# Rows of two tiles in sixteen quads fetched one by one from SyncE and ScalarE in a two-layer relational graph convolution

## The chip, the cores and the metric

The kernel runs on one core of one Trainium2 chip. The metric is the device time in microseconds (us) of one execution; the time of a kernel is the median of its runs. The engines are PE (TensorE), DVE (VectorE), ACT (ScalarE), POOL (GpSimd) and SP (SyncE). SP computes nothing: it issues transfers. ACT and POOL can issue transfers too.

## The reference, cut to what matters

There are 12500 nodes with 128 features, 200000 edges sorted by destination, 8 relations and two layers. Each layer takes, for each destination node, the mean over each relation of the messages that arrive, and sums the means:

```python
W = jnp.einsum('rb,bio->rio', comp, basis)
xw = jnp.einsum('ni,rio->nro', x, W)
msgs = xw[src, et]
seg = dst * N_REL + et
summed = segment_sum(msgs, seg); cnt = segment_sum(ones, seg)
agg = (summed / maximum(cnt, 1)).reshape(N_NODES, N_REL, HIDDEN).sum(axis=1)
h_new = relu(agg + x @ root + bias);  h = h_new + h          # per layer
out = layernorm(x + h)
```

## The kernel before

The edges stand in 1563 tiles of 128 (the last has 64); Q = 4 tiles are a quad (NQ = 391 quads) and G = 8 tiles a group. For every tile the rows of its 128 source nodes must come into the 128 partitions of a buffer of the SBUF. `gather` does that on POOL: one indirect transfer a tile (line 583), at the row numbers that stand in one column of `idx` (layer 1, source x) or `idy` (layer 2, source y_d), and after each a memset of the tile `pace` (line 589), which nothing reads. A ring of 14 buffers of one quad each lets gathers go AHEAD = 12 quads ahead of their use.

Layer 1: for each tile DVE builds a one-hot matrix `dm` (`onehot`, line 873), weighted with the reciprocal counts; PE multiplies rows and `dm` into `s` (`means`, line 914); ACT copies `s` to `sT` (line 568, the helper `copy`); `product` (line 938) multiplies by the eight relation matrices into `y`; `place` (line 961) adds the result to its block of 128 nodes. `close_block` finishes a block: bias, relu and residual on DVE, a transpose (`turn`), the store of the transposed block to `hT_d`, then two halves (`half`, line 986) which multiply the block by all relation matrices of layer 2, and the store of 8 x 128 values a node to `y_d`. `open_block` and `turn_block` bring in the block's root part.

Layer 2 gathers rows of `y_d` (row = node x 8 + relation), so that each tile needs one matmul (`add_rows`, line 1028), accumulated over the tiles of a block; `finish` and `norm` do the rest and store `out`. The first gather of layer 2 waits for the stores of all blocks of `y_d`.

The order of the work is that of the program text: every helper (`vec`, `act`, `pe`, `pool`, `load`) adds an instruction to a list, `Plan`, which works out the semaphore waits by what each one reads and writes, and each engine runs its own instructions in the order of the list. Transfers of `load` (line 565) go out on SP, or at the start on ACT. A transfer takes one of a fixed number of semaphores (a "lane"), in turn, and waits for the lane's previous transfer. The main loop over the quads of layer 1 starts at line 1117, what follows it at 1148, layer 2 at 1160. Other lists that matter: `todo` holds the steps `turn`, `half(0)`, `half(1)` of closed blocks, one of which is taken in most quads. `src_i` holds the source node of each edge with 128 edges of a tile along a row: tile i is row i % 128 of block i // 128; `idx` is its transpose.

After the last instruction all engines meet, POOL drains (line 1185), and a flag `bad` is loaded into a register of every engine (line 1212): if the edges broke an assumption, a general path would run. It doesn't here.

Of the kernel before, what the change touches and what calls it, by code (L numbers as in the profile page):

```python
# [415 lines left out]
def ordered_path(  # L416
# [21 lines left out]

    nc = tc.nc
    P = 128
    N, D = x.shape
# [16 lines left out]
    C = P + 2 * HALO  # L460
    S4 = 4
    AHEAD = 12
    H = R // 2
    assert D == P and R * K == P and B == BF + 1 and 1 < TL and LAST < P and BF % 4 == 0
    main = slice(HALO, HALO + P)

    const = ctx.enter_context(tc.tile_pool(name="const", bufs=1))
# [36 lines left out]
    sel = keep([P, G, K], F32, "sel")  # L504
    spread = keep([P, B, GB], F32, "spread")

    PACE, PACED = 8, (2 * P, 200)
    pace = keep([P, PACE, 2 * P], F32, "pace")
    paced = tc.alloc_semaphore("s_paced")
    key = keep([P, 4, C], F16, "key")  # L510
    low = keep([P, 4, C], I32, "low")
    eqs = Ring(const, 2, [P, S4, 4, C], F16, "eq")
    turns = Ring(const, 3, [P, 4, P], F32, "tu")
    rows_r = Ring(const, AHEAD + 2, [P, Q, D], F32, "rows")
    dm_r = Ring(const, 4, [P, Q, 2 * P], F32, "dm")
    sT_r = Ring(const, 3, [P, R, G, K], F32, "sT")
    pl_r = Ring(const, 3, [P, 2 * P], F32, "pl")
# [27 lines left out]
    o2 = keep([P, B], F32, "o2")  # L545
    nb_f = keep([1, 1], F32, "nb_f")

    plan = Plan(tc, {"hw": 8, "aq": 4, "gq": 3})
    plan.seen, plan.last = {}, {}

    def vec(emit, reads=(), writes=()):
# [15 lines left out]
    def copy(out_t, in_t, reads, writes):  # L567
        act(lambda: nc.scalar.activation(out_t, in_t, AF.Copy), reads, writes)  # L568

    rows_g = {}  # L570

    def gather(l, q):
        if q >= NQ:
            return
        t, cell = rows_r.take()
        rows_g[l, q] = (t, cell)
        ids = idx if l == 0 else idy

        def emit():
            ins = []  # L580
            for i in range(q * Q, min((q + 1) * Q, T)):
                m = LAST if i == T - 1 else P
                ins.append(nc.gpsimd.indirect_dma_start(  # L583
                    out=t[:m, i - q * Q, :], out_offset=None, in_=x if l == 0 else y_d,
                    in_offset=bass.IndirectOffsetOnAxis(ap=ids[:m, i:i + 1], axis=0)))
                k = l * T + i
                if k >= PACE:
                    nc.gpsimd.wait_ge(paced, k - PACE + 1)
                nc.gpsimd.memset(pace[:, k % PACE, :PACED[l]], 0).then_inc(paced, 1)  # L589
            return ins  # L590

        b = q * Q // P
        reads = ["idx0" if l == 0 and q == 0 else ("idx", b)] if l == 0 else [("idy", b)]
        if l == 1 and q == 0:
            reads += [("y_d", j) for j in range(NT)]
        plan.add("POOL", emit, reads, [cell], lane="gq", n=min(Q, T - q * Q))

    def weight(l, r):
        c0 = (l * R + r) * NB
# [306 lines left out]
    def means(q):  # L906
        t, c = rows_g.pop((0, q))
        d, dc = dms.pop((0, q))
        s, sc = s_b[q % 2]

        def emit():
            for i in range(in_quad(q)):
                m = LAST if q * Q + i == T - 1 else P
                last = nc.tensor.matmul(s[:, i, :], t[:m, i, :], d[:m, i, :P], start=True, stop=True)  # L914
            return last

        pe(emit, [c, dc], [sc])
        g = q * Q // G
        if g not in sT:
            sT[g] = sT_r.take()  # L920
        o, oc = sT[g]
        k0 = q * Q - g * G
        n = in_quad(q)
        copy(o[:, :, k0:k0 + n, :].rearrange("p r t k -> p t r k"),
             s[:, :n, :].rearrange("p t (r k) -> p t r k", k=K), [sc], [oc + (q % 2,)])
# [43 lines left out]
    def close_block(j):  # L969
        n = rows_of(j)  # L970
        p, pc = po[j]
        t, c = h_in.pop(j)
        h, hc = h_r.take()
        vec(lambda: nc.vector.tensor_add(h[:n], p[:n], bias_sb[:n]), [pc, "bias"], [hc])  # L974
        vec(lambda: nc.vector.scalar_tensor_tensor(h[:n], h[:n], 0.0, t[:n], op0=ALU.max, op1=ALU.add), [c], [hc])
        pt, pc2 = pt_b
        yc, ycc = yc_r.take()
        yr, yrc = yr_r.take()

        def turn():  # L980
            pe(lambda: nc.tensor.transpose(pt[:, 0, :n], h[:n, :], ident[:n, :n]), [hc, "ident"], [pc2])
            copy(yc[:, :n], pt[:, 0, :n], [pc2], [ycc])
            load(hT_d[j * P:(j + 1) * P, :n], yc[:, :n], [ycc], [("hT_d", j)])

        def half(k):
            pe(lambda: nc.tensor.matmul(pt[:n].rearrange("p r d -> p (r d)"), yc[:, :n],  # L986
                                        w_sb[:, 1, k * H:(k + 1) * H, :].rearrange("p r d -> p (r d)"),
                                        start=True, stop=True),
               [ycc] + [("w", 1, r) for r in range(k * H, (k + 1) * H)], [pc2])
            copy(yr[:n, k * H:(k + 1) * H, :], pt[:n], [pc2], [yrc + (k,)])  # L990
            if k == 1:
                load(y_d[j * P * R:(j * P + n) * R, :].rearrange("(p r) d -> p (r d)", r=R),
                     yr[:n].rearrange("p r d -> p (r d)"), [yrc + (0,), yrc + (1,)], [("y_d", j)])

        todo.extend([turn, lambda: half(0), lambda: half(1)])
# [7 lines left out]
             (ct_b[0].rearrange("p t d -> p (t d)")[:, :2 * P], ct_b[1])]  # L1003

    def load2(k):
        if not 0 <= k < NT:
            return
        n = rows_of(k)
        t, c = hTs[k] = hin_r.take()
        load(t[:, :n], hT_d[k * P:(k + 1) * P, :n], [("hT_d", k)], [c])  # L1010
        t, c = xs[k] = xs_r.take()
        load(t[:n], x[k * P:k * P + n, :], [], [c])

    def add_rows(q, k, opens, last):
# [2 lines left out]
        a, ac = acc[k]  # L1017
        n = in_quad(q)
        root_in = opens and k >= 0
        reads = [c, dc]  # L1020
        if root_in:
            ht, hc = hTs[k]
            reads += [hc, ("w", 1, R)]
# [1 line left out]
        def emit():  # L1025
            for i in range(n):
                m = LAST if q * Q + i == T - 1 else P
                ins = nc.tensor.matmul(a, t[:m, i, :], d[:m, i, :], start=(opens and i == 0),  # L1028
                                       stop=(last and i == n - 1))
                if i == 0 and root_in:  # L1030
                    nc.tensor.matmul(a[:, :rows_of(k)], w_sb[:, 1, R, :], ht[:, :rows_of(k)], start=False, stop=False)
# [63 lines left out]
        gather(0, q)  # L1095
    load_block(0)
    load_block(1)
    run(counts(0), 99)
    sources(*groups[1])
    turn_block(0)  # L1100
# [13 lines left out]
    later = [lambda b=b: check_edges(b) for b in range(B)]  # L1114
    later += [check_span, check_place, check_all]
    later.reverse()
    for q in range(NQ):
        g = q * Q // G
        gather(0, q + AHEAD)
        onehot(0, q + 2)  # L1120
        if q == 1:
            where()
# [8 lines left out]
        else:  # L1131
# [3 lines left out]
            for j in fresh(g):  # L1135
                if j not in hT:
                    turn_block(j)
                load_block(j + 1)
        if q % 4 != 3 and todo:
            todo.pop(0)()  # L1140
        if q < R:
# [3 lines left out]
                parts = None  # L1145
        elif later:
            later.pop()()
    g = NG - 1
    for j in place(g - 1):
        close_block(j)  # L1150
    product(g)
    place_in(g)
    while todo:
        todo.pop(0)()
    for j in place(g):
        close_block(j)
    while todo:
# [2 lines left out]
    for q in range(AHEAD):  # L1160
        gather(1, q)
    load2(0)
    for q in range(2):
        onehot(1, q)
    due = []
    for q in range(NQ):
        k = sup(q)
        gather(1, q + AHEAD)
        onehot(1, q + 2)
        opens = q == 0 or sup(q - 1) != k  # L1170
        last = q == NQ - 1 or sup(q + 1) != k
        if opens:
            acc[k] = acc_b[k % 3]
            load2(k + 1)
        add_rows(q, k, opens, last)
        for d in due:
            norm(d)
        due = []
        if last:
            finish(k)  # L1180
            due.append(k)
# [60 lines left out]
```

## Time and profile before

| | |
|---|---|
| median of 3 runs | 4566.05 us (4556.4 to 4580.39) |
| profiled execution | 4497.58 us |
| span of its instructions | 4495.7 us |
| POOL busy | 3928.1 us (87%) |
| PE busy | 2752.1 us (61%) |
| DVE busy | 1711.8 us (38%) |
| ACT busy | 518.9 us (12%) |
| indirect transfers of a tile, each layer | 1563 |
| DMA share: indirect queue, hardware queue 1 | 17.5%, 5.9% |
| moved | 295.88 MB, mean 66 GB/s |

The page's first part gives each engine's busy time; the second cuts the span in 40 slices with the busy share of each in tenths; the chain follows the work that ended last back from the end, at each step to what released it. In the groups, each line names the code line, engine, operation, output and inputs, how often, then the busy time and the mean of one in ns, and last the idle time ahead of them and what ended most of it. A name with a q (SPq, ACTq, POOLq) is the engine's own queue of instructions: transfers that it issues, register work and waits. "issue" is time in which an engine waited for nothing that the profile shows.

### The profile page before, as it was taken

To read this page: it belongs to the slowest core of one execution; us is meant where nothing else is said; L and a number is where in the kernel's file an instruction comes from. 1 tells how busy PE (TensorE), PEld (TensorE's weight loads), DVE (VectorE), ACT (ScalarE), POOL (GpSimd) and SP (SyncE) were. 2 spreads that over 40 slices of the span, in tenths; PEclk is the share of its full clock that TensorE was granted. 3 is DMA by queue.
4 is the path that set the end of the run, shared out by engine and by line. 5 is a ranking of instruction groups with operands and counts; after the bars stand their busy time and mean duration, and the time that the engine had idled before them with its cause. 6 is when DMAs were issued, how large, how long until landed. Compare 5 with 4: busy or idle time off the path is not lost.

```text
span 4495.7 us, 38109 instructions
## 1 busy us (share of the span) xinstructions
PE 2752.1 (61%) x11691; PEld 2130.6 (47%) x11691; DVE 1711.8 (38%) x4724; ACT 518.9 (12%) x1190; POOL 3928.1 (87%) x6260
## 2 busy tenths in 40 slices
PE   4786666666666666666656565565655556555554
PEld 3565555555555555555544444444444444444443
DVE  8772222222222222222234444444444444444343
ACT  0231121112111111121110000000000000000000
POOL 8888888888888888888878888888888888888886
PEclk7998888888888887888876666666666666666677
DMA  3232222222222222222222222222222222222221
GB/s 90 68 89 73 75 75 75 75 75 75 70 75 75 75 75 75 75 74 72 75 64 56 56 56 56 56 56 56 56 56 56 56 56 56 56 56 56 56 56 44
DMA packets 193416, 295.88 MB, mean 66 GB/s; under 512 B 60725, under 2 KB 130687, under 8 KB 193203
## 3 DMA queue, kind: packets, MB, share of 16 engines
q0 software_dynamic: 100032, 205.00, 17.5%
q1 hardware_dynamic: 90650, 86.62, 5.9%
q8 instruction: 96, 1.57, 0.2%
q10 hardware_dynamic: 2521, 1.73, 0.1%
q14 instruction: 117, 0.96, 0.1%
HBM read 229.11 MB, written 64.00 MB: 65 GB/s over the span
## 4 chain that ended last, share of the span: by engine, by line
POOL 72%; issue 10%; PE 10%; DVE 4%; DMA 4%; ACT 0%; POOLq 0%; ACTq 0%; DVEq 0%; SPq 0%
POOL rows L583 55%; POOL pace L589 17%; PE y L938 3%; DMA rows<-in_x_dram,idx 2%; PE s L914 2%; PE s L1028 2%; DMA rows<-y_d,idy 1%; DVE w_sb L607 1%; PE ct L1028 1%; DVE dm L873 1%; DVE eq L709 1%; PE ct L715 1%; PE ct L716 1%; PE pt L986 0%; DVE tu L732 0%
## 5 line engine op out<-in xcount | busy, mean ns | idle before, releaser
L583 POOL DMA_INDIRECT rows<-y_d,idy x1563 | 1486.6, 951 | 280.2 <-issue 254.8
L583 POOL DMA_INDIRECT rows<-in_x_dram,idx x1563 | 1494.5, 956 | 258.8 <-issue 249.5
L1028 PE MATMUL s<-dm,rows 128*128 128x256 f32 x2086 | 840.8, 567 | 599.1 <-DMA rows<-y_d,idy 445.9
L914 PE MATMUL s<-dm,rows 128*128 128x128 f32 x3126 | 539.7, 326 | 714.7 <-DMA rows<-in_x_dram,idx 714.4
L1028 PEld LDWEIGHTS s<-dm,rows 128*128 128x128 f32 x2086 | 560.9, 285 | 842.4 <-issue 444.1
L589 POOL MEMSET pace<- 128x256 f32 (+1 forms) x3126 | 953.3, 305 | 1.9
L914 PEld LDWEIGHTS s<-dm,rows 128*128 128x128 f32 x3126 | 467.1, 228 | 896.2 <-DMA rows<-in_x_dram,idx 760.1
L873 DVE TENSOR_SCALAR dm<-cols,near,w 128x256 f32<-128x256 f32 x1563 | 725.8, 534 | 56.4 <-PE ct L1028 28.9
L873 DVE TENSOR_SCALAR dm<-cols,kr,w 128x128 f32<-128x128 f32 x1563 | 531.4, 402 | 468.7 <-PE s L914 468.7
L1028 PE MATMUL ct<-dm,rows 128*128 128x256 f32 x1040 | 412.9, 560 | 306.0 <-DMA rows<-y_d,idy 235.0
L938 PE MATMUL y<-w_sb,sT 128*128 128x128 f32 x3136 | 562.1, 356 | 0.0
L938 PEld LDWEIGHTS y<-w_sb,sT 128*128 128x128 f32 x3136 | 553.0, 273 | 0.3 <-issue 0.2
L1028 PEld LDWEIGHTS ct<-dm,rows 128*128 128x128 f32 x1040 | 276.7, 282 | 427.5 <-issue 230.0
L974 DVE TENSOR_TENSOR h<-po,bias_sb 128x128 f32<-128x128 f32 x98 | 28.5, 291 | 944.7 <-PE po L961 944.7
L568 ACT ACTIVATE sT<-s 128x512 f32<-128x512 f32 x391 | 233.3, 597 | 1190.1 <-PE s L914 1189.5
L1047 DVE TENSOR_TENSOR y_col<-s,hT 128x128 f32<-128x128 f32 x66 | 19.2, 291 | 605.0 <-ACT hT L1040 605.0
L986 PE MATMUL pt<-w_sb,y_col 128*128 128x512 f32 x392 | 210.2, 618 | 2.1 <-ACT y_row L568 1.4
L1063 DVE TENSOR_TENSOR h<-po,xs 128x128 f32<-128x128 f32 x98 | 28.6, 292 | 303.8 <-PE po L1062 303.8
L1040 ACT ACTIVATE hT<-s,bias_t 128x128 f32<-128x128 f32 x65 | 23.9, 367 | 997.5 <-PE s L1028 997.5
L568 ACT ACTIVATE y_row<-pt 128x512 f32<-128x512 f32 x196 | 117.0, 597 | 140.4 <-PE pt L986 140.4
L961 PE MATMUL po<-ys,pl 128*128 128x128 f32 x780 | 119.8, 276 | 5.3 <-DVE pl L949 3.1
L1047 DVE TENSOR_TENSOR y_col<-ct,hT 128x128 f32<-128x128 f32 x32 | 9.3, 292 | 291.8 <-ACT hT L1040 291.8
(121 smaller groups left out, 1301.1 us busy)
## 6 DMA issues: line engine op xcount, KB each, us to landing
y_d<-y_row SPq DMA_DIRECT2D x97, 512.0 KB
rows<-in_x_dram,idx POOLq DMA_INDIRECT x1563
rows<-y_d,idy POOLq DMA_INDIRECT x1563
h_in<-in_x_dram SPq DMA_DIRECT2D x98, 64.0 KB
h_in<-hT_d SPq DMA_DIRECT2D x98, 64.0 KB
xs<-in_x_dram SPq DMA_DIRECT2D x98, 64.0 KB
hT_d<-y_col SPq DMA_DIRECT2D x97, 64.0 KB
out_dram<-ys SPq DMA_DIRECT2D x97, 64.0 KB
```

Of the source, the lines that this page charges most:

```text
L568: act(lambda: nc.scalar.activation(out_t, in_t, AF.Copy), reads, writes)
L583: ins.append(nc.gpsimd.indirect_dma_start(out=t[:m, i - q * Q, :], out_offset=None, in_=x if l == 0 else y_d, in_offset=bass.IndirectOffse ...
L589: nc.gpsimd.memset(pace[:, k % PACE, :PACED[l]], 0).then_inc(paced, 1)
L607: vec(lambda b=b: nc.vector.scalar_tensor_tensor(w_sb[:, l, r, :], b_sb[:, l, b, :], comp_sb[:, c0 + b:c0 + b + 1], w_sb[:, l, r, :], op0= ...
L709: vec(lambda s=s, eq=eq, s0=s0: nc.vector.tensor_tensor(eq[:, s - s0, :nb, HALO - s:HALO + P], key[:, :nb, HALO - s:HALO + P], key[:, :nb, ...
L715: nc.tensor.matmul(ct[:, :nb, :], id_h, eq[:, s - s0, :nb, main], start=(s == 1), stop=False)
L873: last = nc.vector.tensor_scalar(t[:, i - q * Q, :wide], cols[:, :wide], ids[:, i:i + 1], w[:, i:i + 1], op0=ALU.is_equal, op1=ALU.mult)
L914: last = nc.tensor.matmul(s[:, i, :], t[:m, i, :], d[:m, i, :P], start=True, stop=True)
L938: last = nc.tensor.matmul(y[:m], t[:, r, :nt, :].rearrange("p t k -> p (t k)"), w_sb[:, 0, r, :], start=(r == 0), stop=(r == R - 1))
L961: last = nc.tensor.matmul(po[j][0][:n], t[:m, k * P:k * P + n], o[:m], start=False, stop=(j in closed))
L986: pe(lambda: nc.tensor.matmul(pt[:n].rearrange("p r d -> p (r d)"), yc[:, :n], w_sb[:, 1, k * H:(k + 1) * H, :].rearrange("p r d -> p (r d)"),
L1028: ins = nc.tensor.matmul(a, t[:m, i, :], d[:m, i, :], start=(opens and i == 0), stop=(last and i == n - 1))
```

## The change

Of every 64 tiles, two no longer come by an indirect transfer from POOL. Tile 63 of the 64 comes over SP and, from the second 64 on, tile 31 over ACT (`far` tells which; in all 24 tiles on SP and 23 on ACT in each layer). `fetch` brings them in bites of 8 rows, one bite on each queue in each quad: the engine loads 8 row numbers from `src_i` into 8 registers, and issues 8 transfers of one row (512 bytes) each at an address from a register; each address takes a fused register instruction ahead of its transfer. A far tile is complete 8 quads (LEAD) before its quad is multiplied. It has a buffer of its own, two for each engine. On ACT in layer 1 the bite is cut in two: register load and 4 rows early in the quad, 4 rows late.

For layer 2 one DVE instruction turns `src_i` into row numbers of `y_d`. The first far tile of each queue in layer 2 waits for all stores of `y_d`.

Besides, the steps at the end of layer 1 stand in another order: `product`, `place` and `close_block` of the group before the last, and all but one of the steps left in `todo`, come ahead of the last quad's `means`. The last block's second half goes to the bank `ct` instead of `pt`, is copied by DVE, and each half is stored by itself. Layer 2 loads two blocks ahead at its start; the last quad's `add_rows` comes after the `norm` of the block before; and POOL gets a drain right after its last gather.

The core of the diff (the reads of `add_rows`, the assertion, and lines that only rename are left out):

```diff
+    FAR, LEAD = 16, 8
+    BITE = P // FAR
+    far_r = {e: Ring(const, 2, [P, D], F32, f"far{e}") for e in ("SP", "ACT")}
-    plan = Plan(tc, {"hw": 8, "aq": 4, "gq": 3})
+    plan = Plan(tc, {"hw": 8, "aq": 4, "gq": 3, "rSP": 4, "rACT": 4})
+    far_at = {"SP": FAR - 1, "ACT": FAR // 2 - 1}
+    row_regs = {e: [plan.engines[e].alloc_register(f"row{k}") for k in range(BITE)] for e in far_at}
+    def far(i):
+        for e, at in far_at.items():
+            if i % (FAR * Q) == at * Q + Q - 1 and i < BF * P and (at == FAR - 1 or i >= FAR * Q):
+                return e
+        return None
+
+    def fetch(e, l, q, part=0, parts=1):
+        s = q + LEAD + FAR - 1 - far_at[e]
+        i, c = (s // FAR * FAR + far_at[e]) * Q + Q - 1, s % FAR
+        if far(i) != e:
+            return
+        if c == 0 and part == 0:
+            far_g[l, i] = far_r[e].take()
+        t, cell = far_g[l, i]
+        n = BITE // parts
+        eng = plan.engines[e]
+        regs = row_regs[e]
+
+        def emit():
+            if part == 0:
+                eng.load(regs, src_i[i % P:i % P + 1, i // P, c * BITE:(c + 1) * BITE])
+            ins = []
+            for k in range(part * n, part * n + n):
+                at = eng.snap(regs[k], min_val=0, max_val=(N if l == 0 else N * R) - 1)
+                p = c * BITE + k
+                ins.append(eng.dma_start(t[p:p + 1, :], (x if l == 0 else y_d)[bass.ds(at, 1), :]))
+            return ins
...
+        tiles = [i for i in range(q * Q, min((q + 1) * Q, T)) if not far(i)]
...
+                rows = far_g[0, q * Q + i][0] if far(q * Q + i) else t[:, i, :]
+                last = nc.tensor.matmul(s[:, i, :], rows[:m], d[:m, i, :P], start=True, stop=True)
...
+            hb, hc2 = ct_b if j == NT - 1 and k == 1 else pt_b
...
+            if j == NT - 1:
+                if k == 0:
+                    copy(yr[:n, :H, :], hb[:n], [hc2], [yrc + (k,)])
+                else:
+                    vec(lambda: nc.vector.tensor_copy(yr[:n, H:, :], hb[:n]), [hc2], [yrc + (k,)])
+                load(y_d[...][:, k * H:(k + 1) * H, :], yr[:n, k * H:(k + 1) * H, :], ...)
+                return
...
+    for s in range(LEAD):
+        fetch("SP", 0, s - LEAD)
+        fetch("ACT", 0, s - LEAD)
...
-    for q in range(NQ):
+    for q in range(NQ - 1):
         g = q * Q // G
         gather(0, q + AHEAD)
+        fetch("SP", 0, q)
+        fetch("ACT", 0, q, 0, 2)
...
+        fetch("ACT", 0, q, 1, 2)
...
+    vec(lambda: nc.vector.scalar_tensor_tensor(src_i[:, :BF], src_i[:, :BF], float(R), ex[:, :BF, main], ...))
     g = NG - 1
+    while todo:
+        todo.pop(0)()
+    place_in(g - 1)
+    for j in fresh(g - 1):
+        open_block(j)
+    product(g - 1)
     for j in place(g - 1):
         close_block(j)
+    place_in(g)
+    while len(todo) > 1:
+        todo.pop(0)()
+    means(NQ - 1)
+    todo.pop(0)()
     product(g)
-    place_in(g)
...
     for q in range(NQ):
         k = sup(q)
         gather(1, q + AHEAD)
+        if q + AHEAD == NQ - 1:
+            pool(lambda: nc.gpsimd.drain())
+        fetch("SP", 1, q)
+        fetch("ACT", 1, q)
         onehot(1, q + 2)
```

## The prediction

> **What bounds the kernel now.** First the page: busy shares, slices, chain and costliest groups.
>
> ```profile
> PE 2752.1 (61%) x11691; PEld 2130.6 (47%) x11691; DVE 1711.8 (38%) x4724; ACT 518.9 (12%) x1190; POOL 3928.1 (87%) x6260
> POOL 8888888888888888888878888888888888888886
> POOL 72%; issue 10%; PE 10%; DVE 4%; DMA 4%; ACT 0%; POOLq 0%; ACTq 0%; DVEq 0%; SPq 0%
> L583 POOL DMA_INDIRECT rows<-y_d,idy x1563 | 1486.6, 951 | 280.2 <-issue 254.8
> L583 POOL DMA_INDIRECT rows<-in_x_dram,idx x1563 | 1494.5, 956 | 258.8 <-issue 249.5
> L589 POOL MEMSET pace<- 128x256 f32 (+1 forms) x3126 | 953.3, 305 | 1.9
> L568 ACT ACTIVATE sT<-s 128x512 f32<-128x512 f32 x391 | 233.3, 597 | 1190.1 <-PE s L914 1189.5
> ```
>
> POOL is busy evenly from start to end; its two gather lines and the pace memset carry the chain. Its idle time is "issue", 0.16 us a gather: it waits for nobody. Next the waits, then POOL in order of time in layer 2.
>
> ```profile
> POOL rows L583 <- issue: 504.3, 3057, 0.2
> POOL rows L583 <- DMA y_d<-y_row: 22.3, 1, 22.3
> ```
> ```profile
> 3000.30 0.95 POOL L583 DMA_INDIRECT rows<-y_d,idy  x1 [0.17 <-issue]
> 3001.25 0.28 POOL L589 MEMSET pace<- 128x200 f32 x1
> 3001.69 0.95 POOL L583 DMA_INDIRECT rows<-y_d,idy  x1 [0.17 <-issue]
> ```
>
> The one real stall is 22.3 us between the layers. The pitch of a gather in layer 2 is (4468.77 - 2288.24)/1562 = 1.396 us by the first and last gathers; in layer 1, by the starts 1435.75 and 1447.28 eight gathers apart, 1.441 us. So a layer is 1563 pitches, and everything else fits under it. SP and ACT have room: ACT is 12% busy and its sT copies wait for PE most of the time, and SP's own waits (2043.7, 1078.5 and 1067.2 us for DVE and ACT results) fill nearly all its time.
>
> The new work needs prices for register loads, register arithmetic and one-partition transfers. The instructions of single lines and of the tiles ex and dx show a few (duration min/median/max in ns):
>
> ```profile
> L1212 SPq TENSOR_LOAD <-bad x1: 467/467/467, 4489.0 to 4489.0; - x1
> L1212 SPq FUSED_REGOPS  x1: 191/191/191, 4493.6 to 4493.6; - x1
> L1185 POOLq DRAIN  x1: 8477/8477/8477, 4480.5 to 4480.5; - x1
> L565 ACTq DMA_DIRECT2D dx<-in_dst_dram x1: 257/257/257, 18.5 to 18.5; - x1
> L565 SPq DMA_DIRECT2D h_in<-hT_d x99: 320/433/459, 2284.9 to 4433.6; - x99
> ```
>
> The 257 ns one is the last dx load, a single partition; the last ex load, also one partition, is the 289 ns minimum of its group. Transfers over 128 partitions take 320 alone and 433 back to back.
>
> [...]the DMA engines are 17.5 + 5.9 + 0.4 = 24% busy.[...]the trace has 467 ns for one register, and no load of eight.[...]
>
> **The change part by part.**
>
> *Gathers removed.* 24 tiles a layer go to SP (63, 127, ... 1535) and 23 to ACT (95, ... 1503). POOL loses 47 gathers and 47 memsets a layer: 47 x 1.441 = 67.7 and 47 x 1.396 = 65.6, together 133 us. POOL's layers become 1516 pitches, 2185 and 2116 us.
>
> *Rows added.* For every quad of four tiles each queue gets one bite: a load of 8 registers, then 8 times a fused register instruction and a one-partition transfer. Call its price F. A row: transfer 0.28 (between 0.257 and 0.289, plus a little for a register address; bounds 0.26 to 0.43), register arithmetic 0.10 (bounds 0.05, near a plain branch at 0.038 to 0.05, and 0.19, the one record, which is the first of its kind after a barrier[...]), two gaps of 0.04 as between SP's back-to-back transfers: 0.46. The load: 1.0 us[...], an estimate. F = 8 x 0.46 + 1.0 = 4.7 us[...].
>
> SP, 384 bites a layer, has besides some 98 x 3 transfers of 0.43 = 126 us: 384 x 4.7 + 126 = 1931, under 2116. ACT, 368 bites, has in layer 1 its copies: sT 233, y_row 117, ys 54, hT 27, y_col 27, together 458 us if nothing overlaps[...]: 368 x 4.7 + 458 = 2188, just at 2185[...]. In layer 2 ACT's copies are 70 us. So both queues fit under POOL, SP at 0.91[...]. The cover is thin: it is gone on SP in layer 2 from F = (2116 - 126)/384 = 5.2, on ACT in layer 1 from 4.7 (serial)[...]. Above that each 0.1 us of F costs 37 to 38 us a layer.
>
> *What is queued behind.* On SP, hT_d, y_d, h_in, xs and out loads stand behind bites, and PE waits for h_in and hT; on ACT, the copies of sT stand behind half a bite (layer 1) and PE waits to reuse s and for product. A layer starts with 8 bites in a row on SP, 8 x 4.7 = 38 us. POOL runs up to 12 quads, about 67 us, ahead of PE, and a far tile is complete 8 quads before its use, so such delays are absorbed if the queues catch up; the last 15 quads of a layer have no bite. Cost nothing while F stays under the limits.
>
> *The wait between layers.* The chain there ran from the last gather at 2264.72 to POOL's restart at 2288.24. Product of the last but one group (3.21), its place and one or two of the y halves now precede the last rows' arrival; the last y goes in two banks with two copies and two stores. What remains after the rows land (2267.06): last means 1.1, one half with 1.2, product 1.9, ys copy and place 0.8, adds 0.6, transpose and copy 0.7, two halves 2.2, copy 0.6, store 3.3, restart 0.7: 2280.2. Gain 8 us, bounds 3 and 11. The DVE multiply of src_i over 1536 columns, about 3 x 0.68 = 2.1 us by the tu group's record, runs while DVE waits for rows. Two moved steps at the end of layer 2 gain about 1 us, not counted.
>
> *The drain.* POOL's drain of 8.5 us starts at 4480.5, after everything, though POOL was done at 4470.0. A drain right after the last gather starts there and ends about 4478.5, beside PE's and DVE's last work; if the second drain finds nothing left, 8 us go. Bounds 0 (the second costs the same) and 9; I take 8[...].
>
> Sum: 133 + 8 + 8 = 149 us; span 4495.7 - 149 = 4347, execution 4497.58 - 149 = 4349. The median of the runs shown, 4566.05, is 1.0152 times the profiled execution; scaled alike, 4415 us, 3.3% faster.
>
> **Rivals.**
>
> *A queue becomes the bound and the kernel is slower.* For it: the only recorded register instruction is 0.19 us[...]. With the row at 0.28 + 0.19 + 0.08 = 0.55 and the load at 1.0, F = 5.4. ACT with serial copies then needs 368 x 5.4 + 458 = 2445 in layer 1, SP 384 x 5.4 + 126 = 2200 in layer 2; with 35 us around the layers (51 before, less 16) the span is 4680, 184 longer, and the time 4753 us. It decides where the sum passes 4495.7: with serial copies at F = (4495.7 - 35 - 458 - 126)/752 = 5.15, with copies that overlap fully (SP alone in both layers) at (4495.7 - 35 - 252)/768 = 5.5.[...] Against it: [...]the copies may overlap.
>
> *Part of the gain is eaten.* F = 5.0 with serial copies on ACT: layer 1 takes 368 x 5.0 + 458 = 2298, layer 2 stays at 2116: 4449, 47 us gained, 4518 us.
>
> *One DMA engine fills up.* If all 12032 rows go to one engine, 2 packets each at the hardware queue's mean (5.9% of 16 x 4495.7, over 90650 packets: 0.047 us) are 1.13 ms, 26% on top of 24%: no bound. It decides from (1 - 0.24) x 4347/12032 = 0.27 us a row; the indirect queue's mean packet, 0.126, would give 0.25. Above it PE waits for rows and the time is over 4566. Few in a hundred.
>
> *The change doesn't do it.* If POOL's pitch were set by how fast transfers drain, fewer gathers would each take longer, leaving the 16 us at the ends: about 4550. Against it: 0.95 + 0.28 + 0.17 makes the pitch, with no wait.
>
> **How the numbers follow.** POOL still sets the time: 0.47, 4415 us, own range 4385 to 4440 (ends' bounds 3 to 20 us). Partly eaten: 0.20, 4440 to 4540. Nothing changed: 0.05. A queue or DMA engine bound, slower: 0.28, of which half lies below 4680. The range 4385 to 4680 leaves about 0.14 above and 0.04 below. The three runs of this kernel lie 0.5% apart, so less than 23 us can't be told from no change: faster 0.67, same 0.05, slower 0.28.
>
> **What would show it.** Right: 1516 gathers a layer at pitches 1.44 and 1.40, no POOL wait longer than the one between layers, and that near 14 us; SP's register instruction near 0.1, its transfer near 0.28, the load near 1.0; a short second drain. Wrong: POOL waiting for PE in each layer's later part, PE waiting for farSP or farACT rows, ACT or SP without idle time[...].

## The result, and the profile after

The changed kernel takes 5226.03 us (median of 4 runs, 5209.97 to 5237.52) against 4568.49 us before (4 runs): a ratio of 1.1437, 95% interval 1.139 to 1.1484. It is 14% slower where 3% faster was forecast. This holds for the chip on which these runs were timed. On another chip the same kernel later took 4370.49 us beside 4498.56, a ratio of 0.9713 (0.9696 to 0.9729). The kernel before splits the chips in the same way: it takes 4556 to 4586 us on some and 4497 to 4500 on others, and nothing between. Below, a chip of the first sort is called tight, one of the second roomy. All executions told of here were recorded by the profiler while they ran. Runs made together, on one chip, are called a job.

The page of the changed kernel, from the tight chip: the span, the busy shares, POOL's slices, the chain by engine and by line, and the two gather groups.

```profile
span 5215.7 us, 75611 instructions
PE 2512.0 (48%) x11691; PEld 2052.8 (39%) x11691; DVE 1710.9 (33%) x4726; ACT 522.6 (10%) x1189; POOL 3819.4 (73%) x6072
POOL 8688888888888888884676667666676666666764
SPq 43%; issue 34%; ACTq 9%; PE 6%; DVE 3%; another core or an unknown queue 2%; ACT 1%; DMA 1%; DVEq 0%
L630 POOL DMA_INDIRECT rows<-y_d,idy x1516 | 1444.9, 953 | 922.0 <-PE po L1121 624.5
L630 POOL DMA_INDIRECT rows<-in_x_dram,idx x1516 | 1454.5, 959 | 418.8 <-issue 214.5
```

POOL's work went as planned: 1516 gathers a layer, each as long as before (953 and 959 ns against 951 and 956). But POOL is no longer in the chain; SP's own queue has 43% of it, and POOL's slices drop from 8 to 6 and 7 in layer 2. Next the waits of several engines, in us in total, times, and the longest; the last line is SP's own longest sum:

```profile
ACT hT L1099 <- DMA farACT<-y_d: 1086.5, 48, 63.9
PE s L1087 <- DMA h_in<-hT_d: 952.8, 53, 20.9
POOL rows L630 <- PE po L1121: 624.5, 91, 33.6
POOL rows L630 <- DMA y_d<-y_row: 59.8, 1, 59.8
SPq L572 <- ACT y_col L575: 61.0, 8, 31.6
```

ACT's copies wait behind the row transfers of its own queue (first line); PE waits for h_in, an ordinary load that stands on SP behind the rows; POOL waits for PE to give buffers back; the wait between the layers grew from 22.3 to 59.8 us. SP itself hardly waits any more: its longest sum is 61.0 us, for y_col, where before it waited over 4000 us in all. So SP's queue sets the pace. The instructions of the row lines on SP tell why (duration min/median/max in ns, then the first and last start):

```profile
L601 SPq TENSOR_LOAD <-src_i x768: 3/734/1677, 18.8 to 5170.6; - x192
L604 SPq FUSED_REGOPS  x6144: 1/44/839, 19.6 to 5174.9; - x199
L606 SPq MOVE farSP<-y_d x3072: 1/29/831, 2431.8 to 5174.9; - x192
L606 SPq DMA_DIRECT2D farSP<-y_d x3072: 1/226/817, 2431.9 to 5175.0; - x192
```

The medians are low: 44 + 29 + 226 ns and the gaps make 0.42 us a row. But the maxima of all four kinds are near 0.8 us or above, even of a MOVE that normally takes 29 ns. The minima are as strange: 2134 of SP's 6144 row transfers are recorded as shorter than 50 ns, where none takes less than 224 in the same kernel on the roomy chip. So the record of an instruction's start may come late, too: an inference from these minima, which no run tested. From the instruction records, the mean distances from one instruction to the next add up to 0.63 us a row in layer 1 and 0.78 in layer 2. In long stretches both SP and ACT advance only once in some 0.70 us, at the same moments, twice in a gather's pitch of 1.39 us, whatever the instruction is: ends on SP at 3023.14, 3024.66, 3025.41, 3026.83 and 3028.26 us, on ACT at 3023.13, 3024.62, 3025.41, 3026.82 and 3028.26. Sorted by what POOL was doing: in layer 2, from one transfer of a bite to the next, a row on SP took 0.93 us while gathers were being issued and 0.42 while none had come for 2 us. First to last gather, layer 1 took 2367.2 us (before 2261.3) and layer 2 2731.1 (before 2180.5).

### The profile page after: what moved, and what is told of

It is laid out like the page before. It is cut to its first block, busy times and chain, and to the rows that moved or that the text cites. A ratio compares the mean times of both kernels' runs of the same rounds, so it can differ in the third digit from the quotient of the medians.

```text
span 5215.7 us, 75611 instructions
## 1 busy us (share of the span) xinstructions
PE 2512.0 (48%) x11691; PEld 2052.8 (39%) x11691; DVE 1710.9 (33%) x4726; ACT 522.6 (10%) x1189; POOL 3819.4 (73%) x6072
## 2 busy tenths in 40 slices
DMA packets 214575, 298.19 MB, mean 57 GB/s; under 512 B 71235, under 2 KB 152973, under 8 KB 214069
## 4 chain that ended last, share of the span: by engine, by line
SPq 43%; issue 34%; ACTq 9%; PE 6%; DVE 3%; another core or an unknown queue 2%; ACT 1%; DMA 1%; DVEq 0%
SPq L606 26%; SPq L604 8%; SPq L601 7%; ACTq L606 6%; SPq L572 2%; ACTq L604 2%; DVE dm L921 1%; PE s L1087 1%; ACTq L601 1%; PE s L963 1%; PE y L987 1%; DVE w_sb L655 1%; DMA h_in<-hT_d 1%; PE pt L1036 1%
## 5 line engine op out<-in xcount | busy, mean ns | idle before, releaser
L630 POOL DMA_INDIRECT rows<-y_d,idy x1516 | 1444.9, 953 | 922.0 <-PE po L1121 624.5
L630 POOL DMA_INDIRECT rows<-in_x_dram,idx x1516 | 1454.5, 959 | 418.8 <-issue 214.5
L1087 PE MATMUL s<-dm,rows 128*128 128x256 f32 x2024 | 626.2, 462 | 1150.6 <-DMA h_in<-hT_d 952.8
L1087 PEld LDWEIGHTS s<-dm,rows 128*128 128x128 f32 x2024 | 453.8, 237 | 1266.1 <-issue 568.0
L1087 PE MATMUL ct<-dm,rows 128*128 128x256 f32 x1008 | 307.6, 457 | 618.8 <-DMA h_in<-hT_d 551.4
L963 PEld LDWEIGHTS s<-dm,rows 128*128 128x128 f32 x3032 | 511.1, 245 | 116.7 <-issue 109.4
L987 PEld LDWEIGHTS y<-w_sb,sT 128*128 128x128 f32 x3136 | 512.4, 255 | 45.4 <-ACT sT L575 23.1
L1087 PEld LDWEIGHTS ct<-dm,rows 128*128 128x128 f32 x1008 | 222.6, 233 | 676.4 <-issue 272.8
L1036 PE MATMUL pt<-w_sb,y_col 128*128 128x512 f32 x390 | 257.0, 746 | 72.5 <-ACT y_col L575 52.6
L1010 PEld LDWEIGHTS po<-ys,pl 128*128 128x128 f32 x780 | 115.2, 212 | 368.5 <-ACT ys L575 289.0
L940 PE MATMUL pt<-ident,h_in 128*128 128x128 f32 x98 | 40.5, 414 | 315.6 <-DMA h_in<-in_x_dram 231.5
```

Of the source, the lines that this page charges most:

```text
L630: ins.append(nc.gpsimd.indirect_dma_start(out=t[:m, i - q * Q, :], out_offset=None, in_=x if l == 0 else y_d, in_offset=bass.IndirectOffse ...
L963: last = nc.tensor.matmul(s[:, i, :], rows[:m], d[:m, i, :P], start=True, stop=True)
L987: last = nc.tensor.matmul(y[:m], t[:, r, :nt, :].rearrange("p t k -> p (t k)"), w_sb[:, 0, r, :], start=(r == 0), stop=(r == R - 1))
L1010: last = nc.tensor.matmul(po[j][0][:n], t[:m, k * P:k * P + n], o[:m], start=False, stop=(j in closed))
L1036: pe(lambda: nc.tensor.matmul(hb[:n].rearrange("p r d -> p (r d)"), yc[:, :n], w_sb[:, 1, k * H:(k + 1) * H, :].rearrange("p r d -> p (r d)"),
L1087: ins = nc.tensor.matmul(a, rows[:m], d[:m, i, :], start=(opens and i == 0), stop=(last and i == n - 1))
```

## The experiments

The theory after this trace (A): the gathers fill something that every instruction of SP and ACT needs as well. The rivals: the rows are simply dearer than priced (B); SP and ACT hinder each other, or the changed ends cost the time; later, that layer 2 is slow for a cause of its own.

**The ends alone, half the rows, SP alone, and prices by stage (tight chip, before 4568.15).** The ends alone:

```diff
     def far(i):
-        for e, at in far_at.items():
-            if i % (FAR * Q) == at * Q + Q - 1 and i < BF * P and (at == FAR - 1 or i >= FAR * Q):
-                return e
         return None
```

> No far tiles at all: all 1563 gathers of a layer stay on POOL, only the other order of the last steps, the split last store and the earlier drain remain. Every theory: layers as before (pitch 1.441 and 1.396 us), wait between the layers near 14 us instead of 22.3, second drain short; 12 to 17 us less than before, ratio 0.996 to 0.998. If the ends carried part of the loss (a new wait between the layers, 59.8 us in the changed kernel), 20 us or more longer than before.

Measured: 4546.58 us, ratio 0.9957 (0.9943 to 0.9971), 22 us less. The ends gain; the loss is the rows'. The run's own trace misses the expectation in two places, though: layer 2 took 2216.3 us and not 1562 x 1.396 = 2181, and the wait between the layers was twice the 14 us expected:

```profile
POOL rows L627 <- DMA y_d<-y_row: 28.0, 1, 28.0
```

No trace of the kernel before from a tight chip was kept, so where the 22 us come from can't be read.

```diff
-    FAR, LEAD = 16, 8
+    FAR, LEAD = 32, 8
```

> FAR = 32: half the rows, bites of 4 on each queue in each quad. Theory A (while POOL issues gathers, each instruction of SP and ACT is held up, so that a row costs 0.75 us in layer 1 and 1.05 in layer 2 instead of 0.42): a bite costs 0.75 + 4 x 1.05 = 4.95 us in layer 2, plus 0.33 for other transfers, 5.3 a quad, just under POOL's 5.5: POOL sets the time, 23.5 gathers a layer saved, 67 us, and 12 to 17 at the ends, ratio 0.98. Theory B (the two queues hold up each other, POOL has no part): the same or better, ratio 0.98. If the hold-up grows when POOL is never idle: 1.00 or more.

Measured: 4612.92 us, ratio 1.0101 (1.008 to 1.0122). Half the rows still lose. While POOL gathered, a row on SP took 0.73 us in layer 1 and 1.3 in layer 2, from transfer to transfer, instead of 0.42.

```diff
-    far_at = {"SP": FAR - 1, "ACT": FAR // 2 - 1}
+    far_at = {"SP": FAR - 1}
...
+        if e not in far_at:
+            return
```

> Only the 24 tiles of SP come row by row; ACT issues none. Theory A: SP's row costs what it cost (layer 2 bound by SP, about 2700 us; layer 1 about 2300), time near 5100. Theory B (SP and ACT hold up each other): SP's row falls to 0.42 us, POOL sets both layers, about 83 us less than before, 4480.

Measured: 4857.75 us (one run), layers of 2303.5 and 2439.4 us. SP has all its rows as before, yet without ACT's more than half of the loss is gone. Neither A nor B as written had that number; what SP's rows cost here depended on what ACT issued at the same time (4857.75 us without ACT's rows, 5226.03 with them).

A kernel of stages then measured the rows by themselves (in outline; the first stage has no gathers):

```diff
+STAGES = [{"quads": 0}, {}, {"memset": 0}, {"gathers": False},
+          {"on": ("SP", "ACT"), "quads": 0}, {"on": ("SP", "ACT")},
+          {"static": True}, {"static": True, "quads": 0}, {"dve": 50}, {"pe": 80}, ...]
```

> No part of the reference is computed: stages one after the other measure 96 rows on SP (12 bites of 8): alone; beside POOL gathers with memsets; beside gathers without memsets; beside memsets alone; on SP and ACT alone; on both beside gathers; at fixed addresses beside gathers and alone; beside gathers and DVE one-hots; beside gathers and matmuls; all together. Theory A: 0.42 us a row alone, 0.7 to 1.05 beside gathers with or without memsets, 0.42 beside memsets alone. Theory B: 0.42 in every SP stage, higher where SP and ACT both issue, POOL or not. Theory C (what holds up SP is DVE or PE work, or trouble with register addresses): 0.42 beside gathers alone, higher only with DVE or PE, or fixed addresses free of it.

Measured, us a row with its share of the load: SP alone 0.522; with gathers and the memset of 200 columns 0.644; with gathers and no memset 1.564; with POOL's memsets and no gathers 0.519; SP and ACT together without gathers 0.526, with gathers 1.45; beside gathers and DVE's one-hots 1.37; beside gathers and PE's matmuls 0.613; at fixed addresses beside gathers 0.294, alone 0.293, though over 28 us only. So the price that I had put on a row was there, SP and ACT didn't hinder each other while POOL didn't gather (0.526), and POOL being busy wasn't enough (0.519 beside its memsets): it took gathers. Beside gathers, ACT's rows (1.45 against 0.644) and DVE's one-hots (1.37) made SP's rows dearer still, while PE's matmuls didn't (0.613). Theory A's 0.7 to 1.05 fits neither the 0.644 nor the 1.564. In the stages that were held up the rows ran at their free price for the first 10 to 20 us and then fell behind, as if something filled up.

**Slower gathers, layer 2's pace, fixed addresses (roomy chip, before 4499.6).**

```diff
-    PACE, PACED = 8, (256, 200)
-    pace = keep([P, PACE, 2 * P], F32, "pace")
+    PACE, PACED = 8, (352, 352)
+    pace = keep([P, PACE, 3 * P], F32, "pace")
```

> The whole change, with POOL's pacing memset widened from 256 and 200 columns to 352 in both layers, so that an undisturbed gather comes every 1.52 us (1.441 at 256 and 1.397 at 200 give 0.0008 us a column) and nothing else is lighter for SP and ACT. Theory A (the gathers fill something that every instruction of SP and ACT needs as well; with fewer gathers a microsecond it has room): the row pitch falls from 0.63 (layer 1) and 0.78 us (layer 2) to 0.42-0.50, SP is no longer the bound, and the time is that of POOL, 1516 x 1.52 = 2300 us a layer, 4640-4720 in all. Theory B (rows cost SP and ACT what they cost whatever the pace of the gathers, since the register instructions are slow in this kernel): SP stays the bound and the time stays at 5150-5250.

```diff
-    PACE, PACED = 8, (256, 200)
+    PACE, PACED = 8, (256, 256)
```

> The whole change, with layer 2's pacing memset at layer 1's 256 columns instead of 200; layer 1 untouched. Theory A: layer 2's length (first to last gather) falls from 2731 us to about layer 1's 2367, because the hold-up follows the pace of the gathers: 4830-4900 in all. If layer 2 is slow for a cause of its own (its rows come from another array, its means and outputs, other work on ACT), layer 2 keeps 2700-2780: 5200-5260.

```diff
-                eng.load(regs, src_i[i % P:i % P + 1, i // P, c * BITE:(c + 1) * BITE])
...
-                at = eng.snap(regs[k], min_val=0, max_val=(N if l == 0 else N * R) - 1)
...
-                ins.append(eng.dma_start(t[p:p + 1, :], (x if l == 0 else y_d)[bass.ds(at, 1), :]))
+                ins.append(eng.dma_start(t[p:p + 1, :], (x if l == 0 else y_d)[p:p + 1, :]))
```

> All rows of the two tiles still come one by one from SP and ACT, but from fixed addresses: no register load, no address arithmetic, one instruction a row instead of three (the row numbers are left out, so these tiles hold other rows). Theory A in the form that it is the count of instructions that overflows: 3072 instead of 9600 a queue and layer are left, SP needs 0.25-0.35 us a row, under 1100 us a layer, and the time is POOL's, 4470-4570. If it is the transfers themselves that are held up (0.33 and 0.63 us more a row, however the address comes): 0.55-0.9 us a row, 4750-5100.

> Nothing of the task is computed. Stages of 40 quads of gathers beside 192 rows from SP (or 128 from SP and from ACT each), then DVE's one-hot operations alone and beside gathers, to map the price of a row against the memset between two gathers. Theory A: a row of SP alone 0.42 between loads; beside gathers with 200 columns it climbs after some 20 us to 0.8 or more, with 256 columns to 0.6, with 352 it stays under 0.5; SP and ACT together are worse than SP alone at 200 and nearly free at 352; rows at fixed addresses on both queues stay at 0.23-0.35 even at 200; DVE's operations slow down beside gathers by a half or more. Theory B: the price doesn't fall with the width of the memset.

Measured (one run each): 4676.01 us with 352 columns, as A expected; 4368.25 at fixed addresses, 100 below A's figure; but 4444.06 with layer 2 at 256 columns, far below what any theory had, and below the kernel before. Layer 1, which that edit doesn't touch, took 2212.6 us instead of 2367.2. So these runs couldn't judge A: there was no hold-up to remove. The stages of m2_micro were built badly: their gathers waited for the rows of their own stage, so nothing overlapped, and they gave prices alone (0.53 us a row). What was left was that this job sat on another chip (theory C: the hold-up belongs to the chip as much as to the kernel).

**The changed kernel itself again (roomy chip, before 4498.56).**

> The changed kernel itself once more, unaltered, beside the kernel before. The last job sat on another chip than the first; the kernel before took 4499.6 us there against 4568 on the first, and even with layer 2's memset at 256 no hold-up was left. Theory C (the hold-up belongs to the chip as much as to the kernel: on some chips the gathers leave less room): if this job's kernel before is near 4500, the changed kernel has rows of 0.42-0.47 us and takes 4370-4430, POOL's 1516 x (1.441 + 1.397) and the ends; if before is near 4565, it takes 5200-5240 again. Theory A (the pace alone decides): 5200-5240 on any chip.

> The whole change with layer 2's memset at 256 columns, as one run before on the other chip (4444 us). Theory C: on a chip with before near 4500 again 4430-4455, some 65 us more than the changed kernel itself, since 1516 x 0.044 us of memset are added and nothing is won; on a chip with before near 4565 layer 2 falls from 2731 us to layer 1's 2367, 4850. Theory A: 4444 on any chip, against 5226 for the changed kernel.

Measured: 4370.49 us (4366.58 to 4372.04), ratio 0.9713 (0.9696 to 0.9729), as theory C said; with 256 columns in layer 2 4444.44, ratio 0.9877 (0.9861 to 0.9894), dearer by 74 us, of which 72 are layer 2's, whose gathers now come every 1.441 us and not every 1.394 (2186.5 - 2114.6). The page of the unaltered changed kernel on this chip, its row instructions on SP, its drain, and its wait between the layers:

```profile
span 4370.3 us, 75611 instructions
PE 2743.0 (63%) x11691; PEld 2124.0 (49%) x11691; DVE 1714.4 (39%) x4726; ACT 517.3 (12%) x1189; POOL 3811.2 (87%) x6072
POOL 8888888888888888888878888888888888888887
POOL 72%; issue 11%; PE 6%; ACTq 4%; DVE 3%; DMA 2%; ACT 1%; POOLq 0%; DVEq 0%; SPq 0%
```
```profile
L601 SPq TENSOR_LOAD <-src_i x768: 712/796/1595, 17.9 to 4273.3; - x192
L604 SPq FUSED_REGOPS  x6144: 44/44/60, 18.6 to 4277.5; - x199
L606 SPq MOVE farSP<-y_d x3072: 29/29/29, 2236.5 to 4277.6; - x192
L606 SPq DMA_DIRECT2D farSP<-y_d x3072: 224/228/299, 2236.6 to 4277.6; - x192
L1251 POOLq DRAIN  x1: 17195/17195/17195, 4343.9 to 4343.9; - x1
```
```profile
POOL rows L630 <- PE s L963: 20.5, 12, 3.8
POOL rows L630 <- DMA y_d<-y_row: 18.3, 1, 18.3
```

The same 75611 instructions, and no hold-up at all: of 6144 register instructions none takes over 60 ns (the longest on the tight chip: 839), of the 3072 MOVEs shown none over 29 (831). POOL is back in the chain and SP out of it.

**Both sorts of chip, quicker gathers.**

```diff
-    PACE, PACED = 8, (256, 200)
+    PACE, PACED = 8, (128, 128)
```

> The whole change with the pacing memset at 128 columns in both layers, a gather every 1.34 us by 0.0008 us a column. Theory C' (the hold-up needs a chip with little room and a quick pace together; two chips with before near 4500 showed none down to 1.394 us): with before near 4500, rows stay at 0.42-0.47 us, SP needs 1730 us a layer of POOL's 2035, and the time is 1516 x 1.34 x 2 and some 60 of ends, 4110-4160, under both kernels; if the room ends between 1.394 and 1.34 us there, rows climb and it takes 4400 or more. With before near 4565: every gather stage quicker than 1.40 us was held up on such a chip, so 5400 or more.

> Nothing of the task is computed. 288 rows from SP beside 160 gathers with memsets of 352, 256, 200, 100 and no columns, then 288 rows on SP and on ACT with 100, rows at fixed addresses on both with 100, and DVE's one-hots beside gathers with 100 and alone. Theory C': on a chip with before near 4500 a row costs SP 0.52 us with its load at every width down to 200, and where the room ends (between 1.39 and 1.25 us a gather, if at all) it climbs within 10-20 us to over 1; on a chip with before near 4565 0.5-0.6 at 352, over 0.6 at 200, over 1.3 without. If nothing climbs at any width on the former chip, the gathers' pace isn't what fills up.

These two fell on a tight chip (before 4581.42): 5685.78 us, ratio 1.2404 (1.2377 to 1.2432). The gathers came 0.06 to 0.11 us quicker than in the changed kernel, and the layers grew by 225 and 243 us, to 2592.1 and 2974.3. Both layers have the same pace here, 1.335 us, and still a row on SP took 0.85 us in layer 1 and 1.20 in layer 2 beside gathers: the pace isn't all, and the rival that layer 2 has a cause of its own besides stays open. m3_micro had m2_micro's fault and gave prices alone: a gather every 1.249 us without a memset, 1.311 at 100 columns, 1.394 at 200, 1.441 at 256, 1.521 at 352. In m4_micro each instruction of a stage waits for the stage before only, so that rows and gathers overlap; the three runs of the next job sat on a roomy chip (before 4496.92).

```diff
-        made.extend(writes)
-        plan.add(e, emit, reads, writes, **kw)
+        mark = ("mark", n_m[0])
+        n_m[0] += 1
+        made.append(mark)
+        plan.add(e, emit, reads, list(writes) + [mark], **kw)
```

> Nothing of the task is computed. In m2_micro and m3_micro the gathers of a stage began only when its rows were done, so they gave each price alone: a row 0.53 us with its load, a gather 1.249 us without a memset, 1.311 at 100 columns, 1.394 at 200, 1.441 at 256, 1.521 at 352. Here they run at the same time: 288 rows from SP beside 160 gathers at each width, then 192 rows on SP and on ACT at 200 columns, 480 on each at fixed addresses, and DVE's one-hots. Theory C' with before near 4570: 0.52-0.60 us a row at 352, 0.60-0.75 at 256 and 200, over 1.0 at 100 and none, SP with ACT at 200 over 1.2. With before near 4500: 0.53-0.56 at 352 to 200, and a climb only at 100 or none, if at all. If the pace of the gathers isn't what decides, no order by width.

> The whole change with 352 columns in both layers, as before. With before near 4570, theory C' (pace and chip together): between 4676 us, the time it took where before took 4500, and 4850, since the hold-up is smaller at 1.52 us than at 1.441, where layer 1 lost 163 us. Theory D (on such a chip rows are held up whatever the pace): 5100-5300. With before near 4500: 4670-4680 again.

> The whole change with 128 columns in both layers, which took 5686 us beside a kernel before of 4581. With before near 4500: 4110-4160 if that chip has room down to 1.335 us a gather, 4400 or more if it ends above. With before near 4570: 5680 again.

Measured: 0.53 us a row at every width, none too, and 0.53 with ACT beside it; one-hots 0.45; 4672.22 us at 352 columns; and 4136.24 at 128 (one run each), in the middle of what was expected of a chip with room. The kernel that is the slowest of all on a tight chip is the fastest on a roomy one, 8% under the kernel before. The last job repeated the stages, with the very same program, and the wide memset, on a tight chip (before 4564.19):

> The same stages as m4_micro, which, beside a kernel before of 4497 us, had rows at 0.53 us at every width of the memset, none too. With before near 4570, theory C' (pace and chip together): 0.52-0.60 us a row at 352 columns, 0.60-0.75 at 256 and 200, over 1.0 at 100 and none, SP with ACT at 200 over 1.2, one-hots at 0.8-1.0 us instead of 0.46. Theory D (on such a chip gathers hold up rows whatever their pace): no order by width, over 0.7 at 352 too. With before near 4500 it repeats m4_micro, 0.53.

> The whole change with 352 columns in both layers, twice 4672 to 4676 us where before took 4497 to 4500. With before near 4570: theory C' 4680-4850, theory D 5100-5300. With before near 4500: 4670-4680.

The row transfers on SP in the stretches in which gathers ran, in m4b_micro at 352, 256, 200, 100 and no columns:

```profile
L208 SPq DMA_DIRECT2D farSP<-in_x_dram x288: 183/225/286, 73.4 to 226.0; - x144
L208 SPq DMA_DIRECT2D farSP<-in_x_dram x288: 2/225/617, 318.9 to 486.4; - x144
L208 SPq DMA_DIRECT2D farSP<-in_x_dram x168: 1/224/1362, 551.0 to 769.9; - x168
L208 SPq DMA_DIRECT2D farSP<-in_x_dram x116: 2/225/704, 840.1 to 1061.7; - x116
L208 SPq DMA_DIRECT2D farSP<-in_x_dram x66: 1/691/991, 1157.0 to 1353.0; - x66
```

The same stretch without a memset in m4_micro, on the roomy chip (the count includes the next stage's first rows):

```profile
L208 SPq DMA_DIRECT2D farSP<-in_x_dram x290: 224/225/271, 987.9 to 1189.7; - x145
```

Divide each stretch by its count: 0.53, 0.58, 1.3, 1.9 and 3.0 us a row, as the gathers come every 1.52, 1.44, 1.39, 1.31 and 1.25 us. Nothing but the memset differs between the stages. The rows are 1.5 us late after some 32 us at 256 columns, 23 at 200, 13 at 100 and 10 at none: the quicker the gathers, the sooner. Once a stage's gathers are done, the remaining rows run at 0.53 again (0.60 after the last of these stages). The order is that of theory C', but not the sizes: 0.60 to 0.75 was expected at 256 and 200 columns. With SP and ACT both at 200 columns a row takes 1.36 us on average, and at fixed addresses, one instruction instead of three, 0.53 where the roomy chip has 0.40; they fall behind only after some 130 us. DVE's one-hots with few rows beside them take 0.47 (0.45 on the roomy chip); that part of the expectation was wrong.

The whole kernel at 352 columns took 4687.15 us on this tight chip (one run), 11 to 15 us more than on the roomy ones. Its chain by engine, and SP's register instructions:

```profile
POOL 50%; issue 15%; PE 12%; SPq 8%; ACTq 7%; another core or an unknown queue 3%; DVE 3%; ACT 2%; DMA 1%; POOLq 0%; DVEq 0%
L604 SPq FUSED_REGOPS  x6144: 1/44/832, 18.0 to 4585.2; - x199
```

The long register instructions are still there, but few enough that SP keeps up: beyond the 0.165 us that stand ahead of every gather, POOL waits 5.5 us in layer 1 and nothing in layer 2, where the changed kernel lost 168 and 613. Together (before is the kernel before in the same job):

| kernel | memset columns | tight: us, before | roomy: us, before |
|---|---|---|---|
| changed kernel | 256, 200 | 5226, 4568 | 4370, 4499 |
| the same, slower gathers | 352, 352 | 4687, 4564 | 4676 and 4672, 4500 and 4497 |
| the same, quicker gathers | 128, 128 | 5686, 4581 | 4136, 4497 |
| ends alone | 256, 200 | 4547, 4568 | not run |

So it takes both: a tight chip, and quick gathers. Beside SP's rows alone there is nothing of it at a gather every 1.52 us (0.53 us a row) and a little at 1.44 (0.58); in the whole kernel some is left at 1.52 (a register instruction of up to 832 ns). On such a chip slower gathers make the kernel faster by 539 us, though POOL then needs more; on a roomy one they make it slower by 300.

What it is that fills up isn't shown. It isn't the load on the DMA engines: while the stage without a memset was held up on the tight chip, they were busy to 20%, and to 21% in the same stage on the roomy one. It isn't how long a gather is on POOL: 953 and 951 ns. A rival that no run tested is the recording itself. The changed kernel's trace holds the records of 75611 instructions and 214575 packets, all four kinds of the row instructions on SP are held up (up to 1677, 839, 831 and 817 ns), and the records of their starts may come late; the writing of records could be what fills up. No execution was timed without being recorded, so it isn't known whether the kernel loses anything on a tight chip when nobody watches. Nor can it be told whether the room belongs to the chip or to the time at which the job ran, since the later jobs each had a chip of their own, visited once.

## Why the prediction was wrong, point by point

**The step that failed** is "Rows added": it took a row's price and set it beside POOL's layer as if the two were independent ("Cost nothing while F stays under the limits", as the next part sums up). The price was not too low. Alone, or on a roomy chip, a bite of 8 rows costs 8 x 0.53 = 4.2 us; forecast 4.7, with the transfer at 0.28 (measured 0.228 on SP, 0.234 on ACT), the register arithmetic at 0.10 (0.044, and a MOVE of 0.029 that I hadn't foreseen) and the load of eight at 1.0 (0.80). With gathers beside it on the tight chip, the layers' lengths give, if SP's queue was full throughout, (2367 - 126)/384 = 5.8 us a bite in layer 1 and (2731 - 126)/384 = 6.8 in layer 2. The limit that I had worked out, 5.2 for SP in layer 2, was crossed by a term that the sum didn't have: what the gathers add to each instruction of the queue. The 1.0 for the load was an estimate, with one record of a single register, 467 ns, behind it; 0.80 us for eight is 0.1 a register.

**The rival that a queue becomes the bound** had the right place and the right sign, and two of the signs named for it came true: POOL waiting for PE in layer 2 (624.5 us), and SP without idle time (its longest sum of waits 61.0 us). One didn't: PE waited for h_in and not for the rows of far tiles. Its reason was wrong. It rested on dear register arithmetic, which costs a quarter of the 0.19 us that it assumed: the one instruction that had 191 ns, at the kernel's end, has 193 in the changed kernel too, those of the rows 44 in the median. And its price, 4753 us at F = 5.4, was too small by 473 us. That copies and rows overlap on ACT, which no record of before showed, is so in the changed kernel: 557 of ACT's 5888 row transfers start while an ACTIVATE runs (on the tight chip), one of 0.23 us at 1003.51, say, inside a copy from 1003.32 to 1003.92. The rival of one DMA engine that fills up falls: a row's transfer is one packet of 512 B, of 25 to 27 ns, and one of 4 B, of 9 ns, and PE never waits for a far tile; whether the rows all go to one engine isn't shown. The rival that POOL's pitch is set by how transfers drain falls: the pitch stayed at 1.441 and 1.394 with 47 gathers fewer.

**The sum of gains** can be tested on the roomy chip, where POOL still sets the time; the profile of before, 4495.7 us, is also such a chip's by its time. Forecast span 4347, measured 4370.3:

| step | forecast | measured |
|---|---|---|
| layer 1, 47 gathers less | 67.7 | 2261.3 - 2213.3 = 48.0 |
| layer 2, 47 gathers less | 65.6 | 2180.5 - 2114.6 = 65.9 |
| between the layers | 8 | 23.5 - 19.6 = 3.9 |
| after the last gather | 8 | 26.9 - 19.3 = 7.6 |
| sum | 149 | 125.4 |

Layer 2 is right to 0.3 us. Layer 1 gives 20 us back: POOL waits 20.5 us for PE, in 12 pieces, nearly all in the first 300 us, where before had none. What delays PE there wasn't tested; at fixed addresses layer 1 gives back 14 us. Between the layers half of what I had counted came (the wait is 18.3 us, not 14). The drain step came to what was forecast: though the drain takes 17.2 us instead of 8.5, it starts with the last gathers, and the second one takes 0.04 us. On the tight chip the step between the layers turned round, to 59.8 us of wait, against 28.0 without rows and 51.7 with half of them: there SP and ACT were late with their rows. That the ends by themselves gain there too, 22 us in all, is shown by the run of them alone.

**Scaling.** I multiplied 4349 by 1.0152, the median over the profiled execution, as if that ratio were noise. It was the one sign of the two sorts of chip in what I had: 4497.58 for the profile against 4556.4 to 4580.39 for the three timed runs, with nothing between, and a gap of 59 us against a spread of 24. I read past it. Even so it couldn't have told the size: the kernel before loses 70 us on a tight chip, the changed kernel 856. The profile of the ends alone, on a tight chip, shows what the small loss looks like: without a single row transfer its layers take 2274.6 and 2216.3 us against 2261.3 and 2180.5.

## What to carry to other kernels

Work moved to an idle queue is priced by what that queue does while the bound engine runs at full pace, not by the durations of its few instructions in quiet stretches (here 0.53 us a row beside up to 3.0): a stage of the new work beside the old gives that price, if it lasts longer than it takes to fall behind, which was 10 to 32 us for these rows and some 130 at fixed addresses. When the profiled execution stands well outside the spread of the timed runs, find out why before scaling by the ratio. Where a kernel fills POOL with gathers, as this one does (87% busy), measure it on more than one chip before keeping a change, and without recording if that can be had: here the wider memset cost 300 us on a roomy chip and gained 539 on a tight one.

## What the runs showed of the hardware that was not expected

- In recorded executions on a tight chip, indirect gathers from POOL slowed the row instructions of SP's and ACT's queues, register arithmetic included (up to 839 and 822 ns in the changed kernel, 44 in the median). In m4b_micro a row on SP went from 0.53 us to 0.58, 1.3, 1.9 and 3.0 as the gathers' pitch went from 1.52 to 1.44, 1.39, 1.31 and 1.25 us. The rows were 1.5 us late 10 to 32 us after the gathers began, the sooner the quicker they came, and ran at 0.53 again (0.60 after the last of these stages) once the gathers were done. In the changed kernel both queues then advance at the same moments, some 0.70 us apart.
- While it lasts, a transfer's record on SP can be 1 to 3 ns long, where the changed kernel undisturbed has none under 224 ns: a recorded duration is then no price.
- It was there on some chips and absent on others (or at some times), with the same program: 5226 or 4370 us. The kernel before differs by only 1.5% between them (4568 and 4499 us).
- A row at an address from a register costs 0.42 us of the queue undisturbed (the changed kernel on the roomy chip): transfer 0.228, register instruction 0.044, MOVE 0.029, the rest gaps. Eight registers from the SBUF take 0.80 us.
- A gather of 128 rows comes every 1.249 us alone (m3_micro); a memset behind it adds 0.06 us at 100 columns, 0.15 at 200, 0.19 at 256 and 0.27 at 352.
